# Attention on one Trainium2 core: VectorE adds the two key halves of every second row, so that its softmax denominators take one matmul pass

## The chip, the core and the metric

The kernel runs on one core of one Trainium2 chip. The metric is device time in microseconds (us), from the first to the last instruction of the program; the kernel before takes 5366.57 us, the median of 3 runs (5366.4 to 5370.02). The engines of a core run in parallel, each through its own list of instructions in order: TensorE (PE in the profile; its weight loads are PEld) for matmuls into PSUM, VectorE (DVE), ScalarE (ACT), GpSimd (POOL), and SyncE (SP), which here only issues transfers.

## What is computed

Four layers act on an image of 256 x 256 pixels with 128 channels, each with a group normalisation ahead and a residual sum behind. Only the first layer, row attention, is changed. For every image row i, with 4 heads of 32 channels:

```python
q, k, v = (zn @ W).reshape(b, n, n, 4, 32)            # of the normalised input
scores = einsum('bijhd,bikhd->bijkh', q, k) / sqrt(32) + bias[:, None]
a = softmax(scores, axis=-2)                          # over the 256 keys k
o = einsum('bijkh,bikhd->bijhd', a, v)
x = x + (sigmoid(zn @ Wg) * o) @ Wo
```

The other layers are a gated linear recurrence of 16 steps, a triangle product and a 3x3 convolution. Everything is in 32-bit floating point.

## The kernel before

The program goes through the layers one after the other: input transposition and statistics, attention in two parts (normalisation and pair bias, then the rows), recurrence, triangle, convolution. The rows of attention are in `attend_bounded` (a runtime flag picks it where the scores are known to be small, so that no maximum is subtracted; that is the case here). It handles the rows i = 0 to 255 in pairs: `rp` counts 128 pairs, with rows a = 2 rp and b = 2 rp + 1.

For one row, the scores are held with the keys on the partitions: 256 keys are two halves `kc` of 128, so a row has 4 heads x 2 halves x 256 queries. The steps and their tiles:

- `project(rp, nm)`: the products `ppq`, `ppk`, `ppv`, `ppg` of a pair in PSUM (one tag `pj` with two buffers, shared with `px`), moved to `tq`, `tk`, `tg` by ScalarE and to `tv` by VectorE.
- `score(i)`: 8 matmuls into two PSUM tiles `sc` (tag `sc`, two buffers in all; one tile holds two heads). Halves run in the outer loop, heads in the inner one, so the first two matmuls write the first tile and the next two the second.
- `biased(i, p2)`: VectorE adds the bias, from a PSUM tile `sc` and `bT` to the SBUF tile `e` of 128 x 1024; this is what frees the `sc` buffer.
- `exponent(i, p2)`: ScalarE takes exp of `e` in place.
- `values(i)`: 16 matmuls into the PSUM tile `nd`: numerators (`tv` with `e`) and denominators (a matrix `ones` with `e`). Each sums the two halves of the keys in PSUM: one matmul a half and head.
- `gated(i)`: VectorE multiplies the denominator by 1 + the gate's exponential into `dn`; `inverse(i)`: ScalarE takes its reciprocal as exp(-ln); `divide(i)`: VectorE multiplies it with the numerator into `og`.
- `output(rp)`: a matmul `px` with the output weights, VectorE's residual sum `x` and its statistics `stats`.

The order on every engine is the order of the code: `mm`, `act_t`, `tt` and the others are wrapped so that the program order is kept. All matmuls are recorded under line 60, ScalarE's activations under line 54, VectorE's operations of this loop under line 476; so groups are told apart by their tiles. A matmul in 32-bit stands in the records as two. The loop works ahead: a pass computes the scores of rows a + 2 and b + 2, the projections of pair rp + 2, the values of rows a and b, and the divisions and output of the pair before. The body of the loop:

```python
for rp in range(N // 2):
    ...
    output(rp - 1)
    if rp == N * 7 // 16:
        self.early_statistics(stats1, "1")
    score(b + 2)
    exponent(a + 2, 1)
    biased(b + 2, 0)
    exponent(b + 2, 0)
    biased(b + 2, 1)
    values(a)
    gated(a)
    inverse(a)
    values(b)
    gated(b)
```

`early_statistics` (lines 119 and 120) is a one-off: in one pass, rp = 112, it aggregates the statistics that are there so far.

Of the kernel before, what the change touches and what calls it, by code (L numbers as in the profile page):

```python
# [9 lines left out]
F32 = mybir.dt.float32  # L10
AF = mybir.ActivationFunctionType
ALU = mybir.AluOpType
# [5 lines left out]
P = 128  # L18
N = 256
NPIX = N * N  # L20
NCH = NPIX // 512
NH, HD = 4, 32
# [8 lines left out]
class Kernel:  # L31
# [27 lines left out]
    def mm(self, out, lhsT, rhs, start=True, stop=True):  # L59
        return self.nc.tensor.matmul(out, lhsT, rhs, start=start, stop=stop)  # L60
# [392 lines left out]
    def attend_bounded(self, xT, x1T, znT, bias, first, w, wb, vb, wo, stats1):  # L453
# [4 lines left out]
        with ExitStack() as c:  # L458
# [8 lines left out]
            ones = cp.tile([P, HD], F32, name="ones")  # L467
# [5 lines left out]
            hp = c.enter_context(self.pool(name="f4", bufs=2))  # L473
# [2 lines left out]
            pin = lambda f: lambda *a, **k: tc.keep_in_program_order(f(*a, **k))  # L476
            mm, act_t, act_i = pin(self.mm), pin(act), pin(self.act)
            tt, stt, bn = pin(V.tensor_tensor), pin(V.scalar_tensor_tensor), pin(V.bn_stats)
            loaded, t, e, nd, dn, og, x1s = {0: first}, {}, {}, {}, {}, {}, {}

            def chunk(rp):

# [11 lines left out]
            def project(rp, nm):  # L494
                if rp >= N // 2:
                    return
                z = chunk(rp)[0]
                o = pj.tile([P, 4, P] if nm == "v" else [P, 512], F32, name="t" + nm)
                if nm == "v":
                    pv = ps.tile([P, 4, P], F32, name="ppv", tag="pj")  # L500
                    for ch in range(4):
                        mm(pv[:, ch, :], z[:, ch * P:(ch + 1) * P], w["v"])
                    tt(o, pv, vb.unsqueeze(1).to_broadcast([P, 4, P]), ALU.add)
                else:
                    pp = ps.tile([P, 512], F32, name="pp" + nm, tag="pj")
                    mm(pp, w[nm], z)
                    if nm == "g":

                        act_t(o, pp, AF.Exp, bias=wb["gn"], scale=-1.0)
                    else:  # L510
                        act_i(o, pp, AF.Identity, bias=wb[nm])
                t[rp, nm] = o

            def score(i):

                if i >= N:
                    return
                q, k, r = t[i // 2, "q"], t[i // 2, "k"], i % 2
                sc = [ps.tile([P, 2, 2, N], F32, name="sc", tag="sc") for _ in range(2)]
                for kc in range(2):  # L520
                    for h in range(NH):
                        hs = slice(h * HD, (h + 1) * HD)
                        mm(sc[h // 2][:, h % 2, kc, :], k[hs, r * N + kc * P:r * N + (kc + 1) * P],
                                q[hs, r * N:(r + 1) * N])
                for p2 in range(2):
                    e[i, p2] = sc[p2]

            def biased(i, p2):
                if i < N:
                    x = hp.tile([P, 2, 2, N], F32, name="e", bufs=8)  # L530
                    tt(x, e[i, p2], bT[:, 2 * p2:2 * p2 + 2], ALU.add)
                    e[i, p2] = x

            def exponent(i, p2):
                if 0 <= i < N:
                    act_t(e[i, p2], e[i, p2], AF.Exp, scale=-1.0)

            def values(i):

                v, r = t[i // 2, "v"], i % 2  # L540
                nd[i] = ps.tile([P, 2, N], F32, name="nd", tag="nd")
                for n in range(2):
                    for kc in range(2):
                        for h in range(NH):
                            hs = slice(h * HD, (h + 1) * HD)
                            lhs = ones if n else v[:, 2 * r + kc, hs]
                            mm(nd[i][hs, n, :], lhs, e[i, h // 2][:, h % 2, kc, :], start=kc == 0, stop=kc == 1)

            def gated(i):

                d = dn[i] = hp.tile([P, N], F32, name="dn")
                g = t[i // 2, "g"][:, (i % 2) * N:(i % 2 + 1) * N]
                stt(d, g, 1.0, nd[i][:, 1, :], ALU.add, ALU.mult)

            def inverse(i):
                if i >= 0:
                    act_t(dn[i], dn[i], AF.Ln)
                    act_t(dn[i], dn[i], AF.Exp, scale=-1.0)

            def divide(i):  # L560
                if i < 0:
                    return
                if i % 2 == 0:
                    og[i // 2] = pj.tile([P, 512], F32, name="og")
                rows = slice((i % 2) * N, (i % 2 + 1) * N)
                tt(og[i // 2][:, rows], nd[i][:, 0, :], dn[i], ALU.mult)

            def output(rp):
                if rp < 0:
                    return  # L570
                xr = chunk(rp)[1]
                if rp % 2 == 0:
                    x1s[rp // 2] = io.tile([P, 1024], F32, name="x1")
                x1 = x1s[rp // 2]
                s = slice((rp % 2) * 512, (rp % 2) * 512 + 512)
                px = ps.tile([P, 512], F32, name="px", tag="pj")
                mm(px, wo["f"], og[rp])
                tt(x1[:, s], px, xr, ALU.add)
                bn(stats1[:, rp, :], x1[:, s])
                if rp % 2 == 1:  # L580
                    nc.gpsimd.dma_start(x1T[:, (rp - 1) * 512:(rp + 1) * 512], x1)
# [21 lines left out]
            for rp in range(N // 2):  # L603
                a, b = 2 * rp, 2 * rp + 1
                score(a + 2)
                inverse(b - 2)
                divide(a - 2)
                biased(a + 2, 0)
                divide(b - 2)
                biased(a + 2, 1)  # L610
                for nm in "qkvg":
                    if nm == "g":
                        exponent(b, 1)
                        exponent(a + 2, 0)
                    project(rp + 2, nm)
                output(rp - 1)
                if rp == N * 7 // 16:
                    self.early_statistics(stats1, "1")
                score(b + 2)
                exponent(a + 2, 1)  # L620
                biased(b + 2, 0)
                exponent(b + 2, 0)
                biased(b + 2, 1)
# [5 lines that stand above are left out]
# [793 lines left out]
```

## Time and profile before

| stretch, us | what | TensorE busy | VectorE busy | ScalarE busy | granted TensorE clock |
|---|---|---|---|---|---|
| 0 to 230 | input | 134.17 | 132.81 | 82.42 | 0.70 |
| 230 to 515 | normalisation, pair bias | 277.28 | 185.57 | 211.88 | 0.98 |
| 515 to 1878 | attention rows | 1357.61 | 1031.65 | 954.32 | 1.00 |
| 1878 to 3400 | recurrence | 1459.98 | 1492.92 | 1443.35 | 0.99 |
| 3400 to 5367 | triangle, convolution | 1902.29 | 1162.54 | 887.72 | 0.99 and 0.98 |

The span of the profiled execution is 5367.2 us. Busy time says how long an engine had something to do in a stretch, not whether another engine waited for it. For that there is the chain of waits: the work that ended last, followed back at each step to what released it. The groups name the time that an engine sat idle before instructions of one kind and what ended the wait. In the groups of the attention rows, the 4096 records `nd<-e,tv` are busy for 271.9 us and the 4096 records `nd<-e,ones` for 268.8 us; four heads' matmuls use different columns of the array and run side by side, so one lasts 0.38 us but they start much closer together. The bias additions `e<-sc,bT` take 1215 ns each on VectorE.

### The profile page before, as it was taken

The numbers are of one execution on the slowest core, as the hardware profiler recorded it, in microseconds if no ns is written. First come the engines' busy times: TensorE is split into PE (matmuls) and PEld (weight loads), VectorE is DVE, ScalarE is ACT, GpSimd is POOL, SyncE is SP. The second block draws the span as 40 slices with busy tenths as digits, with TensorE's granted clock in tenths as the row PEclk, the third lists the DMA queues.
The fourth block names the chain that finished last, engine by engine and source line by source line (L and its number), as shares of the span: only waits on it lengthen the run. The fifth ranks groups of instructions, "written<-read, shape, count | busy, mean of one in ns | idle before, by whom it ended". The sixth has DMA issues, their size and how long they took to land.

```text
span 5367.2 us, 79719 instructions
## 1 busy us (share of the span) xinstructions
PE 5131.3 (96%) x32117; PEld 2871.9 (54%) x32117; DVE 4005.5 (75%) x5023; ACT 3579.7 (67%) x4923; POOL 267.5 (5%) x488
## 2 busy tenths in 40 slices
PE   5699999999999989999999999899999999999999
PEld 4434555555555533333333333338999954339999
DVE  5666777777777779999999999655334526669886
ACT  4376767777776689999999999784333357772210
POOL 1100000000000000000000000000110010000000
PEclk7799999999999989999999999999999999999999
DMA  8875222222222122222222221577667668864331
GB/s 294 331 267 187 68 80 76 72 80 76 72 76 74 57 76 68 72 68 68 68 72 68 68 68 64 207 283 264 230 234 254 234 248 302 295 228 183 141 130 72
DMA packets 185936, 788.84 MB, mean 147 GB/s; under 512 B 36083, under 2 KB 39432, under 8 KB 136384
## 3 DMA queue, kind: packets, MB, share of 16 engines
q1 hardware_dynamic: 120212, 514.73, 29.3%
q0 software_dynamic: 60416, 268.46, 12.4%
q8 instruction: 256, 4.19, 0.3%
q10 hardware_dynamic: 4936, 0.50, 0.1%
q14 instruction: 116, 0.95, 0.1%
HBM read 512.28 MB, written 271.32 MB: 146 GB/s over the span
## 4 chain that ended last, share of the span: by engine, by line
PE 53%; DVE 31%; issue 11%; ACT 2%; DMA 1%; POOL 1%; POOLq 0%; ACTq 0%; DVEq 0%; SPq 0%
PE z L60 9%; PE nd L60 9%; PE m L60 7%; PE sc L60 5%; PE po L60 4%; PE zc L60 4%; DVE tr L796 3%; DVE t L793 3%; DVE y L793 3%; DVE p L793 3%; DVE yf L793 3%; PE ppv L60 3%; PE ppq L60 3%; PE px L60 3%; PE ppk L60 2%
## 5 line engine op out<-in xcount | busy, mean ns | idle before, releaser
L54 ACT ACTIVATE e<-e 128x1024 f32<-128x1024 f32 x512 | 525.4, 1051 | 195.0 <-DVE e L476 194.7
L476 DVE TENSOR_TENSOR e<-sc,bT 128x1024 f32<-128x1024 f32 x512 | 611.5, 1215 | 39.8 <-PE sc L60 39.8
L956 DVE TENSOR_TENSOR LR<-z,sg 128x512 f32<-128x512 f32 x256 | 268.5, 1050 | 363.3 <-ACT sg L54 358.3
L60 PE MATMUL m<-U,v 128*128 128x128 f32 x4608 | 516.5, 276 | 6.6 <-DVE v L1271 6.6
L60 PEld LDWEIGHTS m<-U,v 128*128 128x128 f32 x4608 | 516.4, 192 | 6.7 <-DVE v L1271 6.7
L60 PE MATMUL z<-wf,zt 128*128 128x128 f32 x4096 | 459.5, 275 | 3.6 <-DVE zn L956 3.6
L60 PEld LDWEIGHTS z<-wf,zt 128*128 128x128 f32 x4096 | 459.3, 192 | 4.6 <-DVE zn L956 4.4
L60 PE MATMUL var<-sq,omat 128*128 128x512 f32 x768 | 360.8, 599 | 1.2 <-ACT rs L54 1.2
L54 ACT ACTIVATE dn<-dn 128x256 f32<-128x256 f32 (+1 forms) x640 | 293.8, 459 | 98.6 <-DVE dn L476 88.5
L54 ACT ACTIVATE sg<-z 128x512 f32<-128x512 f32 x256 | 152.8, 597 | 306.6 <-PE z L60 306.6
L54 ACT ACTIVATE rs<-var,eps 128x1024 f32<-128x1024 f32 x192 | 213.4, 1111 | 168.2 <-PE var L60 168.2
L60 PE MATMUL sc<-tq,tk 32*128 32x256 f32 x4096 | 297.7, 402 | 4.5 <-DVE e L476 4.5
L60 PEld LDWEIGHTS sc<-tq,tk 32*128 32x128 f32 x4096 | 187.0, 185 | 161.0 <-issue 147.2
L60 PE MATMUL nd<-e,tv 128*32 128x256 f32 x4096 | 271.9, 383 | 0.0
L60 PE MATMUL nd<-e,ones 128*32 128x256 f32 x4096 | 268.8, 380 | 0.0
L60 PE MATMUL zc<-xin,lc 128*128 128x512 f32 x512 | 248.8, 610 | 6.1 <-DVE zn L956 5.6
L60 PEld LDWEIGHTS var<-sq,omat 128*128 128x128 f32 x768 | 137.9, 189 | 203.8 <-issue 155.2
L60 PE MATMUL av<-y,ident 128*128 128x512 f32 x384 | 192.2, 609 | 44.1 <-DVE y L793 44.0
L60 PE MATMUL po<-LR 128*128 128x256 f32 x1024 | 222.2, 380 | 7.0 <-DVE LR L956 7.0
L60 PEld LDWEIGHTS po<-LR 128*128 128x128 f32 x1024 | 194.1, 190 | 34.2 <-DVE LR L956 7.7
L1308 ACT COPY m4s<-m 128x512 f32<-128x512 f32 x32 | 18.7, 584 | 285.4 <-PE m L60 285.4
L54 ACT ACTIVATE rs<-rs 128x1024 f32<-128x1024 f32 x192 | 202.9, 1057 | 6.1
(325 smaller groups left out, 10095.0 us busy)
## 6 DMA issues: line engine op xcount, KB each, us to landing
zt<-znT SPq DMA_DIRECT2D x128, 1024.0 KB
znT<-zn POOLq DMA_DIRECT2D x64, 1024.0 KB, 5.7
xin<-x2T SPq DMA_DIRECT2D x64, 1024.0 KB
xr<-x3T SPq DMA_DIRECT2D x46, 768.0 KB
xin<-in_x_dram SPq DMA_DIRECT2D x64, 512.0 KB
xT<-xo POOLq DMA_DIRECT2D x64, 512.0 KB, 10.4
xr<-xT SPq DMA_DIRECT2D x64, 512.0 KB
xin<-xT SPq DMA_DIRECT2D x32, 1024.0 KB
```

The source lines that it names most:

```text
L54: return self.nc.scalar.activation(out, in_, func, bias=bias, scale=scale, **kw)
L60: return self.nc.tensor.matmul(out, lhsT, rhs, start=start, stop=stop)
L476: pin = lambda f: lambda *a, **k: tc.keep_in_program_order(f(*a, **k))
L793: pin(V.tensor_tensor(out, a, b_, op))
L796: pin(V.scalar_tensor_tensor(out, a, k, b_, op0, op1))
L956: pin = lambda f: lambda *a, **k: tc.keep_in_program_order(f(*a, **k))
L1308: nc.scalar.copy(m4, m[4])
```

## The change

For row b of each pair, and not for row a, VectorE adds the two halves of the keys of the exponentials `e` into a new SBUF tile `es` (two instructions a row, 128 x 512 each). The denominators of this row then need one matmul a head instead of two: 4 fewer a pass. Row a keeps 8. The matmuls of `values` are also written in two loops instead of one, in the same order as before. `es` has two buffers. The additions stand in VectorE's order where `fold(b)` is called: behind the statistics of `output`, ahead of the bias additions of row b + 2. The purpose is to take work from TensorE and give it to VectorE.

```diff
+            def fold(i):
+                x = es[i] = hp.tile([P, NH, N], F32, name="es")
+                for p2 in range(2):
+                    y = e[i, p2]
+                    tt(x[:, 2 * p2:2 * p2 + 2], y[:, :, 0, :], y[:, :, 1, :], ALU.add)
+
             def values(i):
                 v, r = t[i // 2, "v"], i % 2
                 nd[i] = ps.tile([P, 2, N], F32, name="nd", tag="nd")
-                for n in range(2):
-                    for kc in range(2):
-                        for h in range(NH):
-                            hs = slice(h * HD, (h + 1) * HD)
-                            lhs = ones if n else v[:, 2 * r + kc, hs]
-                            mm(nd[i][hs, n, :], lhs, e[i, h // 2][:, h % 2, kc, :], start=kc == 0, stop=kc == 1)
+                for kc in range(2):
+                    for h in range(NH):
+                        hs = slice(h * HD, (h + 1) * HD)
+                        mm(nd[i][hs, 0, :], v[:, 2 * r + kc, hs], e[i, h // 2][:, h % 2, kc, :], start=kc == 0, stop=kc == 1)
+                folded = i in es
+                for kc in range(1 if folded else 2):
+                    for h in range(NH):
+                        hs = slice(h * HD, (h + 1) * HD)
+                        mm(nd[i][hs, 1, :], ones, es[i][:, h] if folded else e[i, h // 2][:, h % 2, kc, :],
+                           start=kc == 0, stop=folded or kc == 1)
...
                 score(b + 2)
                 exponent(a + 2, 1)
+                fold(b)
                 biased(b + 2, 0)
                 exponent(b + 2, 0)
                 biased(b + 2, 1)
```

More of the change, by code (lines that the diff above doesn't have):

```diff
@@ L478, in attend_bounded @@
             tt, stt, bn = pin(V.tensor_tensor), pin(V.scalar_tensor_tensor), pin(V.bn_stats)
-            loaded, t, e, nd, dn, og, x1s = {0: first}, {}, {}, {}, {}, {}, {}
+            loaded, t, e, es, nd, dn, og, x1s = {0: first}, {}, {}, {}, {}, {}, {}, {}
             def chunk(rp):
```

## The prediction

> **What bounds the kernel now.** I read the view by stages first, since the change touches only the attention loop, then the chain of waits in order of time, then VectorE's own timeline. The attention stage in the view by stages (columns: stretch, length, then busy time and count of TensorE, its weight loads, VectorE, ScalarE and GpSimd, granted clock, DMA share, GB/s):
>
> ```profile
> 520.00:1878.00 1358.00, 1352.61 (x14245) 709.88 (x14244) 1029.33 (x1397) 952.15 (x1395) 33.65 (x63) 1.00 0.24 73
> ```
>
> TensorE is busy all the time, VectorE 76%, ScalarE 70%. The chain of waits, in order of time, has nothing but TensorE; one pass of the loop (start, length, piece):
>
> ```profile
> 1308.01 1.08 PE sc L60 x16
> 1309.09 3.59 PE nd L60 x64
> 1312.68 1.08 PE sc L60 x16
> 1313.76 1.05 PE ppq L60 x2
> 1314.81 0.86 PE ppk L60 x2
> 1315.67 1.08 PE ppv L60 x8
> 1316.75 0.86 PE ppg L60 x2
> 1317.61 1.05 PE px L60 x2
> ```
>
> These eight pieces make a pass of 10.65 us (10.64 from one `px` to the next). So at present time taken from TensorE is time won, as long as nothing else sets the pass. VectorE in the same pass, in the timeline:
>
> ```profile
> 1308.05 0.69 DVE L476 TENSOR_TENSOR x<-px,xr 128x512 f32<-128x512 f32 x1 [1.22 <-PE px L60]
> 1308.78 0.69 DVE L476 BATCH_NORM_STATS2 stats<-x 128x6 f32<-128x512 f32 x1
> 1309.39 2.34 DVE L476 TENSOR_TENSOR e<-sc,bT 128x1024 f32<-128x1024 f32 x2
> 1311.64 0.41 DVE L476 SCALAR_TENSOR_TENSOR dn<-tg,nd 128x256 f32<-128x256 f32 x1
> 1312.75 0.42 DVE L476 SCALAR_TENSOR_TENSOR dn<-tg,nd 128x256 f32<-128x256 f32 x1 [0.70 <-PE nd L60]
> ```
>
> What to see: after `px`, VectorE adds the residual, takes statistics and does the two bias additions; these end at 1309.39 + 2.34 = 1311.73. They free the two `sc` buffers in PSUM that TensorE writes next, at 1312.61. So the VectorE way has only 0.88 us to spare in a pass, though the engine is idle for a quarter of the time. The idle 1.22 us lies ahead of `x`, before this stretch.
>
> **A disturbance in the same place.** In one pass (row pair 112) the early statistics, 3.36 us of VectorE work, are queued exactly where the change puts its two additions: behind `stats`, ahead of the bias additions. VectorE, then TensorE, in the timeline:
>
> ```profile
> 1713.97 3.19 DVE L119 BATCH_NORM_AGGREGATE early<-stats 128x2 f32<-128x672 f32 x1
> 1717.19 0.17 DVE L120 TENSOR_SCALAR early<-early 128x2 f32<-128x2 f32 x1
> 1717.27 2.35 DVE L476 TENSOR_TENSOR e<-sc,bT 128x1024 f32<-128x1024 f32 x2
> 1719.53 0.74 DVE L476 SCALAR_TENSOR_TENSOR dn<-tg,nd 128x256 f32<-128x256 f32 x2
> 1720.87 0.42 DVE L476 TENSOR_TENSOR og<-nd,dn 128x256 f32<-128x256 f32 x1 [0.60 <-ACT dn L54]
> 1721.21 1.22 DVE L476 TENSOR_TENSOR e<-sc,bT 128x1024 f32<-128x1024 f32 x1
> 1722.34 0.41 DVE L476 TENSOR_TENSOR og<-nd,dn 128x256 f32<-128x256 f32 x1
> 1722.67 1.22 DVE L476 TENSOR_TENSOR e<-sc,bT 128x1024 f32<-128x1024 f32 x1
> ```
> ```profile
> 1718.54 0.70 PE L60 MATMUL sc<-tq,tk 32*128 32x256 f32 x4 [1.40 <-DVE e L476]
> 1719.67 2.08 PE L60 MATMUL sc<-tq,tk 32*128 32x256 f32 x12 [0.43 <-DVE e L476]
> ```
>
> Here the VectorE way shows itself. The first 4 of 16 `sc` records start when the first bias addition has freed its buffer, the other 12 when the second has (1719.62, then 1719.67). The rest of the pass can be read off relative to B = 1719.62, the end of the second addition: the two `dn` at B - 0.09, `og` at B + 1.25 after ScalarE's logarithm and exponential, bias additions at B + 1.59 and B + 3.05.
>
> [...] in the recurrence, 128x512 additions and products in SBUF last 0.69 us and start 0.60 us apart when queued (2001.33, 2001.93, 2002.53). [...] it granted 0.50 from 1719.46 to 1726.29, after a window with 1.79 of 3.41 us busy.
>
> **The change, part by part.**
> - Removed: 4 of 32 `nd` matmuls in a pass, 8 of 64 records (each matmul is two). Blocks of 16 records start 0.86 us apart (1309.91, 1310.77, 1311.63), so 0.43 us. TensorE's own sum falls to 10.64 - 0.43 = 10.21.
> - Added: two 128x512 additions on VectorE, 2 x 0.60 = 1.20 us in a pass. The strided halves (256 elements in a run) I price like contiguous ones; the other bound is 0.69 each plus a start gap of 0.04, that is 1.46.
> - Their inputs: the last exponential of row b is done at about 1306.7, before `x`, so they wait for nothing. The `ones` matmuls of row b wait for them, but come last in `nd`, some 2.7 us after its start; free. The 2 extra buffers of `es` were read a pass or more before; free.
> - The order: the additions stand behind `stats` and ahead of the bias additions. Behind them are queued the bias additions of row b + 2 (TensorE's next `sc` waits for their buffers), then `dn`, `og` and the next bias additions.
>
> Now the VectorE way through a pass, from B to the next B: bias additions at B + 1.59 and + 3.05 as above; `tv` next, 1.13 later as in a pair of additions: + 4.18, done at + 4.87; `px` starts 0.06 after `tv`, as it does now (1306.83, 1306.89; they share a PSUM tag): + 4.93; `x` comes 1.16 after `px` (1306.89, 1308.05): + 6.09; bias additions 1.34 after `x`, plus the fold's 1.20: + 8.63; done 2.34 later: + 10.97. Without the fold it is 9.77, which agrees with the slack seen: 10.64 - 9.77 = 0.87. TensorE's way through the same pass is shorter: B + 0.05, 12 records of `sc` at 1.08/16 each, 0.81; `ppq` to `px` 3.85 as now (1303.04, 1306.89), so `px` could start at B + 4.71, and the pass would be 4.71 + 1.16 + 1.34 + 1.20 + 2.34 = 10.75.
>
> So the pass goes from 10.64 to the largest of 10.21, 10.75 and 10.97: 0.33 longer. It does so in the passes with an `x`, 126 of them: 126 x 0.33 = 42 us. 5366.6 + 42 = 5408.
>
> **The rivals.**
> - *Hidden* (faster): the fold falls into VectorE's idle time and TensorE's matmuls still set the pass. 128 x 0.43 = 55 less: 5312. For it: VectorE is idle 2.5 us in a pass. Against it: the idle time lies ahead of `x` and of `dn`, and the 0.88 us behind `stats` is less than 1.20. It needs a fold below about 0.45 us to gain anything.
> - *Only the short way* (slightly slower): `tv` is not late, and the pass is 10.75: 126 x 0.11 = 14, 5380. For it: the difference, 0.22, is a small sum of many gaps. Against it: pass 112 shows the long way's starts directly.
> - *No change*: needs 0.33 of my sum to be wrong, all in one direction; 5367.
> - *Costlier fold*: 1.46 instead of 1.20: 11.23, 126 x 0.59 = 74, 5441.
> - *Clock* (much slower): TensorE, now idle about 0.8 us a pass, is throttled. In pass 112 a wait of 3.36 - 0.88 = 2.5 us became 16.24 - 10.64 = 5.6 us (the `sc` of row b + 2 starts at 1712.40 and next at 1728.64), 3.1 of it from the halved clock. Were one pass in three hit so, 42 x 3.1 = 130 more: about 5540. Against it: [...] the recurrence with TensorE gaps of 0.61 us shows clock 1.00 from 2000 to 3200.
>
> **How the numbers follow.** Long way near 10.97: 0.60; short way: 0.15; costlier fold: 0.08; clock: 0.03; no change: 0.06; hidden: 0.08. The range reaches from the short way to the costlier fold, 5380 to 5440; outside are hidden, no change and clock, 0.17. Slower by over 0.2%: 0.60 + 0.15 + 0.08 + 0.03 = 0.86.
>
> **What would show it.** Right: `sc` starts about 10.97 apart, TensorE idle ahead of the last 12 `sc` records about 0.5 us in nearly every pass with VectorE's `e` as the releaser, a wait of `og` for ScalarE of about 0.6, none of `dn` for `nd`, an `es` group of x256 near 0.69 us, clock still 1.00. Wrong: a chain in the loop of TensorE alone (hidden), or clock 0.50 in the loop (clock). `px` right behind `ppg` would mean the short way.

## The result, and the profile after

| | time, us (median) | ratio to the kernel before, 95% interval |
|---|---|---|
| before | 5368.30 | |
| changed | 5413.57 | 1.0084 [1.0066, 1.0101] |

The change makes the kernel slower by 45 us; the interval is 35 to 54 us. The time is lost in the attention rows alone, which now last from 520 to 1923 us. In the view by stages:

```profile
520.00:1923.00 1403.00, 1383.32 (x13232) 710.39 (x13230) 1164.68 (x1654) 940.46 (x1398) 33.55 (x63) 1.00 0.23 70
```

TensorE's records fell by some 1,000 and still cover 98.6% of the stretch, VectorE rose from 76% to 83%. This view does not tell who sets the pass. The chain of waits, in order of time, tells more (its limits show in the second experiment); it was of TensorE alone, and one pass of it now reads

```profile
1308.35 0.04 issue
1308.40 1.13 PE sc L60 x12
1309.53 1.06 PE ppq L60 x2
1310.59 0.86 PE ppk L60 x2
1311.44 1.08 PE ppv L60 x8
1312.52 0.86 PE ppg L60 x2
1313.38 1.06 PE px L60 x2
...
1314.47 0.70 DVE x L476
...
1315.19 0.69 DVE stats L476
1315.89 1.19 DVE es L476 x2
1317.08 2.28 DVE e L476 x2
```

From the end of one pair of bias additions `e` (1308.35) to that of the next (1317.08 + 2.28 = 1319.36) it is 11.01 us, where it was 10.64. `nd`, TensorE's largest piece and the one that the change cut, is no longer on the chain: VectorE's `x`, `stats`, `es` and `e` stand in its place, with the two additions at 1.19. VectorE's own timeline of the same pass:

```profile
1308.26 0.74 DVE L476 SCALAR_TENSOR_TENSOR dn<-tg,nd 128x256 f32<-128x256 f32 x2
1309.60 0.42 DVE L476 TENSOR_TENSOR og<-nd,dn 128x256 f32<-128x256 f32 x1 [0.60 <-ACT dn L54]
1309.94 1.21 DVE L476 TENSOR_TENSOR e<-sc,bT 128x1024 f32<-128x1024 f32 x1
...
1311.40 1.21 DVE L476 TENSOR_TENSOR e<-sc,bT 128x1024 f32<-128x1024 f32 x1
1312.56 0.69 DVE L476 TENSOR_TENSOR tv<-ppv,vb 128x512 f32<-128x512 f32 x1
1314.47 0.69 DVE L476 TENSOR_TENSOR x<-px,xr 128x512 f32<-128x512 f32 x1 [1.22 <-PE px L60]
1315.19 0.69 DVE L476 BATCH_NORM_STATS2 stats<-x 128x6 f32<-128x512 f32 x1
1315.80 1.28 DVE L476 TENSOR_TENSOR es<-e 128x512 f32<-128x512 f32 x2
1317.00 2.35 DVE L476 TENSOR_TENSOR e<-sc,bT 128x1024 f32<-128x1024 f32 x2
```

The 1.22 us of idle time ahead of `x` is still there, unused, and the additions follow behind it. What TensorE loses shows in its weight loads (PEld) for the second group of scores and in the start of the product `ppq` behind them, first in the kernel before, then in the changed one:

```profile
1312.61 0.74 PEld L60 LDWEIGHTS sc<-tq,tk 32*128 32x128 f32 x16 [0.41 <-issue]
1313.69 1.12 PE L60 MATMUL ppq<-zn,wq 128*128 128x512 f32 x2
```
```profile
1307.59 0.30 PEld L60 LDWEIGHTS sc<-tq,tk 32*128 32x128 f32 x4 [0.41 <-DVE e L476]
1308.39 0.73 PEld L60 LDWEIGHTS sc<-tq,tk 32*128 32x128 f32 x12 [0.50 <-DVE e L476]
1309.46 1.12 PE L60 MATMUL ppq<-zn,wq 128*128 128x512 f32 x2
...
1313.31 1.12 PE L60 MATMUL px<-og,wo 128*128 128x512 f32 x2
```

Before, `ppq` starts 1.08 us behind the start of the group; now it starts 1309.46 - 1307.59 = 1.87 behind it. The 0.79 between them is the whole of what TensorE now loses in a pass, 11.00 - 10.21: the new wait is 0.50, and the 12 records left behind it take nearly as long as all 16 did (more on this below). The waits of the stage (who waited for whom: total, times, longest), before and changed:

```profile
DVE dn L476 <- PE nd L60: 91.4, 128, 1.8
...
PEld sc L60 <- DVE e L476: 2.7, 2, 1.9
```
```profile
PEld sc L60 <- DVE e L476: 115.2, 250, 1.0
...
DVE dn L476 <- PE nd L60: 1.7, 3, 0.8
```

The weight loads for the scores waited for VectorE's bias additions twice in the whole stage; now it is 250 times, twice a pass. Only one of the two is new: the loads of the first 4 records also sat idle for 0.41 us before, for no visible reason (`issue`). VectorE's wait for `nd`, 91.4 us before, is 1.7.

The sum over the stage: from the first `x` to the last it was 1881.1 - 531.1 = 1350.0 us and is 1925.5 - 533.4 = 1392.1, so 42.1 more. The starts of `x` in the two traces show where: 123 regular passes of 11.00 us instead of 10.64 are 44 more, the pass with the early statistics gave 1.8 back (below), and the last three, in which projections and scores run out, take 24.6 us together, as before. The loop starts 2.3 us later, which the change does not reach; with this it is 44.4, where the two profiled spans differ by 44.1.

### The profile page after: what moved, and what is told of

It is laid out like the page before. It is cut to its first block, busy times and chain, and to the rows that moved or that the text cites. A ratio compares the mean times of both kernels' runs of the same rounds, so it can differ in the third digit from the quotient of the medians.

```text
span 5411.3 us, 77926 instructions
## 1 busy us (share of the span) xinstructions
PE 5159.2 (95%) x31093; PEld 2871.4 (53%) x31093; DVE 4139.3 (76%) x5279; ACT 3565.9 (66%) x4923; POOL 266.7 (5%) x488
## 4 chain that ended last, share of the span: by engine, by line
DVE 42%; PE 41%; issue 12%; ACT 2%; DMA 1%; POOL 1%; SPq 0%; POOLq 0%; ACTq 0%; DVEq 0%
PE z L60 9%; PE m L60 7%; DVE e L476 5%; PE po L60 4%; PE zc L60 3%; DVE tr L808 3%; DVE es L476 3%; PE sc L60 3%; DVE t L805 3%; DVE y L805 3%; DVE p L805 3%; DVE yf L805 3%; PE ppv L60 3%; PE px L60 3%; PE ppq L60 2%
## 5 line engine op out<-in xcount | busy, mean ns | idle before, releaser
L60 PE MATMUL sc<-tq,tk 32*128 32x256 f32 x4096 | 382.9, 409 | 16.1 <-DVE e L476 3.6
L60 PEld LDWEIGHTS sc<-tq,tk 32*128 32x128 f32 x4096 | 220.9, 184 | 223.9 <-DVE e L476 119.7
L54 ACT ACTIVATE dn<-dn 128x256 f32<-128x256 f32 (+1 forms) x640 | 280.0, 456 | 65.2 <-DVE dn L476 55.0
L476 DVE TENSOR_TENSOR x<-px,xr 128x512 f32<-128x512 f32 x128 | 88.4, 691 | 154.7 <-PE px L60 154.6
```

The costliest lines, as they stand in the source:

```text
L54: return self.nc.scalar.activation(out, in_, func, bias=bias, scale=scale, **kw)
```

## The experiments

Theory: the pass is set by a closed way, bias additions - scores - projections - `px` - `x` - statistics - bias additions, of which VectorE's queue behind `px` is a part; the change adds 1.20 us to it where 0.87 are free. Rivals: VectorE simply has too much work; the two parts of the change each cost and gain on their own; the new wait of `nd` for `es`.

### The additions ahead of the residual sum

```diff
+                fold(b)
                 output(rp - 1)
...
                 exponent(a + 2, 1)
-                fold(b)
                 biased(b + 2, 0)
```

> The changed kernel, with the two additions queued on VectorE ahead of the residual sum x instead of behind its statistics. Theory (the place in the queue costs the time): there VectorE waits 1.22 us for px in every pass, and the additions take 1.20, so the way from x to the next scores is 9.80 us a pass again and TensorE's own sum, 10.64 - 0.43 = 10.21, sets the pass: 126 x 0.43 = 54 us less than the kernel before, about 5314 us. Rival (the amount of VectorE work costs the time, wherever it stands): no gain over the changed kernel, about 5413 us. Also shown right: VectorE's idle time before x nearly gone, chain in the loop of TensorE alone.

Measured: 5317.1 us, ratio 0.9907 [0.9890, 0.9923]. The same instructions, moved by two places in one queue, ahead of `x` and `stats`, turn a loss of 45 us into a gain of 50. VectorE's timeline:

```profile
1307.03 0.69 DVE L476 TENSOR_TENSOR tv<-ppv,vb 128x512 f32<-128x512 f32 x1 [0.31 <-PE ppv L60]
1307.64 1.28 DVE L476 TENSOR_TENSOR es<-e 128x512 f32<-128x512 f32 x2
1308.94 0.69 DVE L476 TENSOR_TENSOR x<-px,xr 128x512 f32<-128x512 f32 x1
```

The additions fill the gap; `x` has no idle time ahead of it. The chain is TensorE's alone again, and a pass is 10.21:

```profile
1309.98 3.16 PE nd L60 x56
1313.14 1.08 PE sc L60 x16
```

`nd` takes 3.16 instead of 3.59, and the scores behind it 1.08, so they wait for nothing. So the amount of work on VectorE is not what costs; its place is.

### The additions alone

```diff
-                folded = i in es
+                folded = False
```

> The changed kernel with the additions made but not used: all 32 matmuls of nd are kept. Theory (VectorE's way of 11.00 us sets the pass, TensorE's sum of 10.64 hides below it): same time as the changed kernel, 5410 to 5417 us, since the removed matmuls saved nothing there. Rival (the two parts add up, the saving of 54 us is real and the additions cost 99): about 5467 us.

Measured: 5417.0 us, ratio 1.0091 [1.0074, 1.0108]. Putting all matmuls back costs nothing that can be told from the changed kernel, so in the changed kernel their removal gained nothing. In the traces the regular pass is 11.00 in both; of the 4.2 us between their spans 3.1 are the one pass with the early statistics. In this kernel `nd` does not use `es` at all, so the new wait of `nd` for `es` is not needed for the loss either. The chain of this kernel, in order of time, holds only TensorE; that VectorE sets the pass shows in one length, and in the timeline:

```profile
1302.41 3.59 PE nd L60 x64
1306.01 1.44 PE sc L60 x16
```
```profile
1303.91 2.35 DVE L476 TENSOR_TENSOR e<-sc,bT 128x1024 f32<-128x1024 f32 x2
...
1307.37 1.12 PE L60 MATMUL ppq<-zn,wq 128*128 128x512 f32 x2
```

`sc` takes 1.44 where it took 1.08 before: the bias additions end at 1303.91 + 2.35 = 1306.26, within the group, its later records need the buffer that they free, and `ppq` follows 1.11 us after that end, as in the changed kernel. In the chain the group's records cover the wait: it shows no idle time from 1306.01 to 1307.44. A chain that holds only TensorE is therefore no proof that TensorE sets the pass; the length of the `sc` group has to be read too.

### The matmuls removed alone

```diff
-                folded = i in es
+                folded = i % 2 == 1
...
-                fold(b)
```

(and `e` in the place of `es` in the matmuls)

> The matmuls removed without the additions: the denominators of row b sum the first half of the keys alone, the second half is left out. Theory (TensorE sets the pass of the kernel before): the pass is 10.21 us, 126 x 0.43 = 54 less than before, about 5314 us. Rival (TensorE is busy but a wait sets the pass of before already): no change, about 5368 us.

Measured: 5315.5 us, ratio 0.9904 [0.9884, 0.9923]. TensorE did set the pass of the kernel before, and one wave of `ones` matmuls is worth 53 us. The first experiment keeps all of it.

### Half of it, by heads

```diff
-                for p2 in range(2):
-                    y = e[i, p2]
-                    tt(x[:, 2 * p2:2 * p2 + 2], y[:, :, 0, :], y[:, :, 1, :], ALU.add)
+                y = e[i, 0]
+                tt(x[:, 0:2], y[:, :, 0, :], y[:, :, 1, :], ALU.add)
```

> Half of the change in the same place: one addition (heads 0 and 1), and 2 matmuls fewer a pass instead of 4. Theory (a slack of about 0.85 us behind the statistics, then every 0.1 us costs 0.1 us): 0.60 fits into the slack, VectorE's way is 10.40 us, TensorE's sum 10.43, and the pass is 0.21 shorter: 126 x 0.21 = 27 less than before, about 5341 us, faster than before though the whole change is slower. Rival (the additions cost in proportion): half of the change's loss, about 5391 us.

Measured: 5371.9 us, ratio 1.0005 [0.9998, 1.0012]: neither. The chain is TensorE's, and tells why:

```profile
1303.53 3.59 PE nd L60 x60
```
```profile
1304.42 2.35 DVE L476 TENSOR_TENSOR e<-sc,bT 128x1024 f32<-128x1024 f32 x2
```

60 records take 3.59 us, as 64 did. The four heads' matmuls run side by side: in TensorE's timeline of this kernel two records of `es` (heads 0 and 1) start at 1306.08 and two of `e` (heads 2 and 3) at 1306.09, 0.39 us long. Heads 2 and 3 still need both halves of the keys, one after the other, and leaving out one half for heads 0 and 1 shortened nothing. Here time was saved by the wave (3.16 for 56 records in the matmuls alone), not by the matmul, and my 0.21 was wrong. The other half of the expectation held: VectorE's bias additions ended at 1304.42 + 2.35 = 1306.77, 0.28 ahead of the start of the scores (1307.05 in TensorE's timeline) instead of 0.88. The 0.60 fitted into the slack.

### Half of it, by queries

```diff
-                    tt(x[:, 2 * p2:2 * p2 + 2], y[:, :, 0, :], y[:, :, 1, :], ALU.add)
+                    tt(x[:, 2 * p2:2 * p2 + 2], y[:, :, 0, :P], y[:, :, 1, :P], ALU.add)
```

(the denominators of queries 0 to 127 take one matmul a head, those of the others two, at 128 columns each)

> Half of the change by queries: the additions cover 128 of the 256 queries of all four heads (two of 128x256), and the denominators of these queries alone take one matmul a head; so a whole wave of four heads is saved, at half the columns. Theory (slack of about 0.85 us behind the statistics): two additions take 2 x 0.33 = 0.67 and fit, VectorE's way is 9.80 + 0.67 = 10.47, TensorE's sum 10.64 - 0.21 = 10.43, the pass 10.47, 126 x 0.17 = 21 us less than before, about 5347 us. Rival (no slack, cost in proportion to the additions): 126 x 0.18 = 23 more, about 5391 us.

Measured: 5350.1 us, ratio 0.9955 [0.9941, 0.9969]. Now whole waves fall, and half of the change in its own unfavourable place makes the kernel faster. The chain of this kernel:

```profile
1301.26 3.38 PE nd L60 x72
1304.64 1.11 PE sc L60 x16
```

72 records in 3.38 us, fewer columns though more matmuls; a pass is 10.47, as worked out, VectorE's 9.80 + 0.67. TensorE's own sum is 10.43, and the missing 0.04 is about what `sc` takes longer (1.11 for 1.08). The cost of the additions is not in proportion: with all matmuls kept, 0.60 was free (the half by heads), and 1.20 costs 0.36, about what exceeds the slack of 0.87. With fewer matmuls TensorE's sum is shorter, and the slack is shorter by as much.

### tv without VectorE

```diff
-                    tt(o, pv, vb.unsqueeze(1).to_broadcast([P, 4, P]), ALU.add)
+                    act_i(o, pv, AF.Identity)
```

> The changed kernel with tv moved out of PSUM by ScalarE, so that px no longer waits for VectorE's queue; the bias row of v (zero in these inputs) is left out. Two ways through the pass came out equal in the changed kernel: VectorE's, with tv done 4.90 us after the bias additions, and TensorE's, whose last 12 score records take 1.06 us instead of the 0.81 of the prediction, which puts px at 4.96 too. Theory (either way alone gives 11.00): same time as the changed kernel, 5410 to 5417 us. Rival (only VectorE's late tv sets the pass, as the prediction had it): 10.75 us a pass, about 5381 us.

Measured: 5404.1 us, ratio 1.0063 [1.0042, 1.0083]; about 9 us below the changed kernel, outside both expectations, and far nearer to the theory's. TensorE's timeline:

```profile
1307.98 1.02 PE L60 MATMUL ppg<-zn,wg 128*128 128x512 f32 x2
1308.84 1.11 PE L60 MATMUL px<-og,wo 128*128 128x512 f32 x2
```

`px` comes 0.86 behind `ppg`, not 0.95, and the pass is 10.90. The 0.1 belongs to the copy of `tv`, which lasts 0.60 on ScalarE and 0.69 on VectorE; `px` starts 0.06 after its end on either. With VectorE's queue out of the way between the bias additions and `px`, the way over TensorE and this copy still takes 10.90. So the lateness of `tv` in VectorE's queue, by which I had the pass, is not needed for the loss. In the changed kernel it was hardly late: VectorE comes free for `tv` just as `ppv` is there. `tv` starts at 1312.56, 0.04 after the last record of `ppv` ends (1311.36 + 1.16 = 1312.52), where it was 0.03 in the kernel before (1306.14 after 1304.95 + 1.16).

### Scores tile by tile

```diff
-                for kc in range(2):
-                    for h in range(NH):
+                for p2 in range(2):
+                    for kc, h in ((0, 2 * p2), (0, 2 * p2 + 1), (1, 2 * p2), (1, 2 * p2 + 1)):
```

> The changed kernel with the 8 score matmuls of a row in another order: all four of the first PSUM tile (heads 0 and 1), then all four of the second. Theory (heads run side by side in rows of the array, and a head's own four records take the time, however many others there are): after the second bias addition 8 records of heads 2 and 3 are left, and ppq starts about 1.1 us after it, as in the changed kernel with 12 left. Rival (time goes with the number of records, 0.067 each, as the prediction had it): ppq starts about 0.6 us after it. The whole time stays near 5413 us either way, since VectorE's way of 11.00 us is not touched.

Measured: 5412.75 us in one run, as expected of both. What tells is the start of `ppq` after the bias additions, in the timeline:

```profile
1304.82 2.35 DVE L476 TENSOR_TENSOR e<-sc,bT 128x1024 f32<-128x1024 f32 x2
...
1308.29 1.12 PE L60 MATMUL ppq<-zn,wq 128*128 128x512 f32 x2
```

1304.82 + 2.35 = 1307.17, and `ppq` starts 1.12 later, with 8 score records left. With 12 left, in the changed kernel, it is 1309.46 - 1308.35 = 1.11. In the kernel before all 16 took 1.07. In these three cases, in each of which two heads or more had their own four records to do, the number left did not matter; fewer than four a head were not tried. The chain of this kernel holds only TensorE, as in the second experiment, though it is as slow as the changed one.

### px ahead of the gate's projection

```diff
-                for nm in "qkvg":
-                    if nm == "g":
-                        exponent(b, 1)
-                        exponent(a + 2, 0)
+                for nm in "qkv":
                     project(rp + 2, nm)
                 output(rp - 1)
+                exponent(b, 1)
+                exponent(a + 2, 0)
+                project(rp + 2, "g")
```

> The changed kernel, additions still behind the statistics, with the output product px and all of output moved ahead of the gate's projection ppg in TensorE's order. Theory (the pass is the way from the bias additions over px and x to the next bias additions): px starts about 0.95 us earlier, the way is 10.05 us, TensorE's sum of 10.21 sets the pass, and about 54 us less than the kernel before, 5314 us. Rival (VectorE's additions have no room behind the statistics, whatever TensorE's order): 5413 us.

Measured: 5312.6 us, ratio 0.9891 [0.9875, 0.9908]. The additions stand where the change put them, behind the statistics, and are free, because everything behind `px` comes earlier. VectorE's timeline:

```profile
1303.76 0.69 DVE L476 TENSOR_TENSOR x<-px,xr 128x512 f32<-128x512 f32 x1 [0.17 <-PE px L60]
...
1305.10 1.27 DVE L476 TENSOR_TENSOR es<-e 128x512 f32<-128x512 f32 x2
1306.29 2.35 DVE L476 TENSOR_TENSOR e<-sc,bT 128x1024 f32<-128x1024 f32 x2
```

VectorE's wait for `px` has shrunk from 1.22 to 0.17, and a pass is 10.21 (`px` at 1302.70 and 1312.91), TensorE's sum. This shows the closed way through `px` from its other side.

### The additions on GpSimd

```diff
-                fold(b)
...
+                fold_g(b)          # the same two additions by nc.gpsimd.tensor_tensor
                 output(rp - 1)
```

> The change with row b's additions on GpSimd instead of VectorE. Theory (the loss of the change is only the 1.20 us in VectorE's queue): VectorE's way is 9.80 again, TensorE's sum of 10.21 sets the pass, about 5314 us, provided that GpSimd ends the additions within some 4 us of the last exponential. Rival (the new wait of the denominators for es, or GpSimd's reads, cost a pass): above 5330 us, with waits of nd for es.

Measured: 5315.0 us, ratio 0.990 [0.988, 0.992]. No wait of `nd` for the sums shows in the loop. In the changed kernel there are only two in the whole stage, 2.7 us together (the loads of `nd` for `es`), so the new wait is not what cost.

### Both rows

```diff
+                fold_g(a)
                 score(a + 2)
...
+                fold(b)
                 output(rp - 1)
```

> Both rows folded: row b by VectorE ahead of the residual sum, as in the first experiment, and row a by GpSimd, which is idle in the loop but for one transfer issue in two passes. TensorE's sum falls by another 0.43 to 9.78, VectorE's way stays 9.80, so if GpSimd is fast enough and disturbs no one: 9.80 a pass, 126 x 0.84 = 106 us less than the kernel before, about 5263 us. Rival (GpSimd slows VectorE's reads of SBUF, or is slower than a pass): no better than the first experiment, 5317 us or more; the lengths of VectorE's groups tell.

Measured: 5267.6 us, ratio 0.9810 [0.9794, 0.9827], the fastest of all. The chain in order of time is of VectorE, with ScalarE's reciprocal; a part of the pass:

```profile
1302.22 0.70 DVE x L476
...
1312.02 0.70 DVE x L476
...
1313.43 2.26 DVE e L476 x2
```

From `x` to `x` it is 9.80, VectorE's way as worked out. TensorE's own sum, worked out as 10.64 - 0.86 = 9.78, lies just below it, so a further gain needs less work on both.

## Why the prediction was right, and where it was not

**Forecast and result.** 42 us slower by 126 passes of 10.97; measured 45, by 123 regular passes of 11.00 (126 were counted; the last three are shorter) and small differences elsewhere.

**VectorE's way, step by step.** The steps that I took from the one disturbed pass came true. In the pass shown above, relative to the end of the bias additions, forecast and measured (B = 1308.35): `og` 1.25 and 1.25; bias additions 1.59 and 1.59, 3.05 and 3.05; `tv` 4.18 and 4.21; `px` 4.93 and 4.96; `x` 6.09 and 6.12; next bias additions 8.63 and 8.65; their end 10.97 and 11.01. The additions cost 1.19 against 1.20; each lasts 0.68 us (679 ns in the mean), and the halves with strides cost no more than the contiguous 128x512 operations of the recurrence (700 ns in the mean for `u<-u,tr` in the kernel before).

**The slack.** 0.87 behind the statistics: the half by heads, 0.60, fitted into it, and the additions alone, 1.20 with all matmuls kept, cost 0.36 a pass for the 0.33 worked out.

**Removed matmuls.** 0.43 a wave: shown by the matmuls alone (53 us for 54). In the changed kernel it bought nothing, as forecast.

**The step that failed.** "TensorE's way through the same pass is shorter: ... 12 records of `sc` at 1.08/16 each, 0.81." They took 1.06 (1308.40 to `ppq` at 1309.46). I divided a wave by the number of its records; heads run side by side, and the time was that of each head's own records (1.07, 1.06 and 1.07 us with 16, 12 and 8 left). A line of the prediction had it already: in pass 112 the 12 records took 2.08 us at a granted clock of 0.50, by which I estimate 2.08 x 0.50 = 1.04 at a clock of 1.00. With 1.06, TensorE's way is 0.05 + 1.06 + 3.85 + 1.16 + 1.34 + 1.20 + 2.34 = 11.00, the same as VectorE's. So the rival "only the short way", 5380, does not exist, and the pass had two ways of equal length. That the error left the number standing is luck: VectorE's way happened to be as long as the true one of TensorE. The reason that I gave, a late `tv`, was at most half of it: `tv` started within 0.04 of the end of `ppv`, as in the kernel before, and moving it off VectorE brought only 0.10 a pass. Pass 112 could not show this: TensorE's granted clock was 0.50 in it. The same error made me expect a gain from leaving out two heads.

**Two lesser errors.** "It needs a fold below about 0.45 us to gain anything": that is the limit for the full gain; some gain is left for any fold below 0.87, and the half by queries, with 0.67 of additions, gained 21 us. And a chain of TensorE alone, which I named as the sign of *hidden*, is no safe sign: the additions alone and the scores tile by tile have such a chain and are as slow as the changed kernel.

**Clock.** 1.00 in the loop (520 to 1923 us), as forecast; the wait of 0.50 us a pass did not lower it in this kernel.

**The other rivals.** Hidden fell with the result, but was one edit away: 5317 us with the additions in the gap, or 5313 with `px` earlier, are its number, 5312. A costlier fold fell with 1.19.

## What to carry to other kernels

An engine that is idle for a quarter of the time has room only where it is idle: before moving work to it, find the gap in its queue, and follow what is queued behind the new instruction to the engine that now sets the pass. A one-off that happens to sit in the same place is a free experiment; its pass shows the chain that the change will bring to the surface, as far as the other engines run in it as usual. The matmuls of heads that ran side by side had to be counted in waves here: fewer of them in a wave saved nothing (3.59 us for 64 records and for 60), and a whole wave less saved 0.43.

## What was not expected of the hardware

- The scores of four heads take the same time with 16, 12 or 8 records left (1.07, 1.06 and 1.07 us to the next product; the last with the 0.05 taken off that TensorE needed to start elsewhere), and `nd` the same with 64 and 60 (3.59).
- In the pass with the early statistics, TensorE's granted clock was 0.50 from 1719.46 to 1726.29 us in the kernel before and 1.00 from 1756 to 1770 in the changed one, though it was idle longer there: 1.73, 0.51 and 0.43 us against 1.40 and 0.43. That pass took 14.43 us instead of 16.24. The view by stages gives 1.00 (third figure from the right) in its two stretches with waits and in the one behind them:

```profile
1756.00:1759.40 3.40, 2.26 (x44) 1.09 (x36) 3.37 (x3) 0.00 (x0) 0.01 (x1) 1.00 0.88 269
1759.40:1762.80 3.40, 1.93 (x12) 0.59 (x12) 3.40 (x5) 1.06 (x1) 0.00 (x0) 1.00 0.10 40
1762.80:1766.20 3.40, 3.35 (x19) 1.76 (x20) 2.80 (x6) 2.51 (x6) 0.00 (x0) 1.00 0.00 0
```

  The waits added up do not decide it: with `px` ahead of the gate's projection TensorE waited for 0.68, 0.51 and 0.43 us in this pass, less than in the changed kernel, and the granted clock was 0.50 behind them:

```profile
1669.68:1673.09 3.41, 3.41 (x14) 1.85 (x15) 2.81 (x6) 1.56 (x4) 0.00 (x0) 0.50 0.00 0
```

  What decides it was not shown.
- GpSimd's additions last 1.27 us (the median with row b's additions on it) and 1.32 us (the mean with both rows, 600 to 1600 us) against 0.68 on VectorE. In the regular passes they hardly changed VectorE's times: with both at work, its additions `es` take 684 ns in the mean (679 in the changed kernel) and its bias additions 1212 (1213). But in the first pass of the kernel with both rows, an addition of VectorE began just after one of GpSimd, at 527.63, and lasted 1.80 us instead of 0.68, past the end of GpSimd's:

```profile
527.03 2.39 DVE L476 TENSOR_TENSOR es<-e 128x512 f32<-128x512 f32 x2
527.59 1.28 POOL L476 TENSOR_TENSOR esg<-e 128x512 f32<-128x512 f32 x1 [9.55 <-ACT e L54]
```

  In the regular pass at 1300 us VectorE's came first, at 1300.91, GpSimd's at 1301.94, and GpSimd's two lasted 2.75 us together. Whether additions on both engines would hold each other up in another order was not tried.
